# First pair of layer 0: projections, values and column sums at other places of the hand-written order

## The chip, the cores and the metric

The kernel runs on one core of a Trainium2 chip. The metric is the device time of one execution in microseconds (us). A core has five engines with queues of their own that run side by side and wait for each other by semaphores: TensorE (PE, matmuls; its weight loads are shown as PEld), VectorE (DVE), ScalarE (ACT), GpSimd (POOL), and SyncE (SP), which here issues the transfers.

## What is computed

Two layers of attention on `x` of 128 x 256 x 256 in float32, each added to its input. The change lies in layer 0 alone:

```python
m_norm = layer_norm(m)                      # m: x after a group norm over 32 groups of channels
q, k, v = m_norm @ Wq.T, m_norm @ Wk.T, m_norm @ Wv.T      # 8 heads of 32
b = layer_norm(z) @ Wb.T                    # a bias for each head, 256 x 256, the same for all rows
gate = sigmoid(m @ Wg.T + bg)
scores = einsum('bsihc,bsjhc->bshij', q, k) * scale + b
p = softmax(scores)
o = einsum('bshij,bsjhc->bsihc', p, v) * gate
x = x + o @ Wo.T + bo
```

`s` runs over 128 rows, `i` and `j` over 256 positions. Layer 1 is a banded attention on the result; nothing of it is changed.

## The kernel before

**The preparation** (up to some 219 us) reads `z` in tiles of 32 positions, forms the bias, and keeps its exponential `eb` in SBUF: exp(score + bias) is taken as exp(score) times `eb`. For a tile, VectorE takes the statistics (`zst`, L1102) and the variance (`zrs`, L1109), and POOL raises it to the power -1/2 (`z_power`, L1116). PE transposes (`z_turn`, L1143), ScalarE copies (`zT`, L1145), PE multiplies by the bias weights (`z_project`, `ps_b`, L1155). After four such steps ScalarE copies `bT` (L1164), PE transposes it back into `ps_k` (L1167), VectorE multiplies by the roots (`z_weigh`, `bt`, L1179), and ScalarE takes the exponential (`z_exp`, `eb`, L1190). Beside it, blocks of `x` are read for the mean and the root of the group norm, `M0` and `R0`.

The last tiles of `z` are woven by hand with the beginning of layer 0, in `last_tiles`. The first pair of rows, `now`, is centred and scaled on POOL (L1283, L1286), has its layer-norm statistics taken by VectorE (`moments`, L1296 to L1302), their roots by POOL (`root`, L1306), and is transposed and projected to q and k. `columns` (L1576) brings `R0` and `M0` from rows to columns: eight small PE records (L1580) and two VectorE instructions (L1584, L1585) into `col`, which pairs from the third on use in `scale_blocks`.

**The main loop** takes two rows (a pair) in each of 64 passes; in pass `p`, `now` is the pair whose scores are made, `nxt` the next, `nn` the one after it, `was` and `old` the two before. q, k and the gate of a pair are projected in two halves (`project(which, m)`, L1364) of four heads each: half 0 is enough for `scores(r, 0)`, half 1 for `scores(r, 1)`; r is the row of the pair. The steps of a pass that matter here:

- `scores(r, c)`: 8 PE matmuls (L1401) into two PSUM tiles of a pool of two, and their exponentials on ScalarE (L1413). For c = 0 the second goes to SBUF, which frees its PSUM tile.
- `add_bias(r, c)`: two products with `eb` on VectorE (`e`, L1421), and two sums over the halves of the positions on POOL (`eboth`, L1425).
- `apply(r)`: products with the values (`ps_ov`, L1436) and sums of the weights from `eboth` (`ps_su`, L1444).
- `values(r)` on PE (L1382) and `keep_values(r)` on VectorE (L1388).
- For the pair to come: `centre` and `scale` on POOL, `moments` on VectorE, `root` on POOL, `send` (a VectorE transpose, L1310, and four transfers to DRAM, L1312), `fetch` (one transfer that spreads these 512 roots over all partitions, `rs_r`, L1319), and `normal` (POOL multiplies `xgT` by `rs_r` to `xnT`, L1351).
- For pair 1, `turn`: eight PE transposes (`ps_x`, L1329) and two ScalarE copies (`xgT`, L1333). Later pairs get `xgT` by a VectorE transpose of blocks that are loaded apart (`blocks`, `turn_blocks`).
- `residual` (POOL, L1289) adds the output bias to the rows.

The order is written out by hand (`tc.manual_schedule`): each engine runs its own instructions in the order of the program text, and waits where an operand isn't there. So a step's place among other steps decides what stands behind it on each of its engines. Projections, values and the small products of `columns` share a pool of two PSUM banks (`mm`); one that finds no free bank waits for the eviction of the product two before.

In pass 0 there are no earlier pairs, so `was` and `old` do nothing, and pair 1 has to be brought from its rows to `xnT` within the pass.

Of the kernel before, what the change touches and what calls it, by code (L numbers as in the profile page):

```python
# [21 lines left out]
def bcast(ap, axis, n):  # L22

    ap = ap.unsqueeze(axis)
    shape = list(ap.shape)
    shape[axis] = n
    return ap.broadcast_to(shape)
# [746 lines left out]
def fast_kernel(  # L774
# [215 lines left out]
    def mm(name):  # L990
        return ps_mm.tile([P, 512], F32, name=name, tag="mm")
# [122 lines left out]
    def z_power():  # L1114
        rs = powers.pop(0)
        nc.gpsimd.tensor_tensor(rs, rs, mhalf[:, : rs.shape[1]], ALU.pow)  # L1116
# [57 lines left out]
    def z_weigh():  # L1174
        b, i0, rs, ps_k = unweighed.pop(0)
        bt = pz.tile([P, IS, H], F32, name="bt", tag="bt", bufs=2)
        for j in range(4):
            q = slice(j * 16, (j + 1) * 16)
            nc.vector.tensor_tensor(  # L1179
                bt[:, q, :].rearrange("p (g a) h -> p g a h", g=4), ps_k[:, :, :, j, :].rearrange("p a g h -> p g a h"),  # L1180
                bcast(rs[:, q].rearrange("p (g a) -> p g a", g=4), 3, H), ALU.mult,
            )
        weighed.append((b, i0, bt))

    def z_exp():

        while weighed:
            b, i0, bt = weighed.pop()
            for h in range(H):
                nc.scalar.activation(  # L1190
                    eb[:, h, :, b * P + i0 // NB : b * P + (i0 + IS) // NB],
                    bt[:, :, h].rearrange("p (u b) -> p b u", b=NB), AF.Exp, bias=bz_r[:, h : h + 1],
                )
# [355 lines left out]
    def pair(p):  # L1549
        return Pair(p) if p < NP else Nobody()  # L1550
# [14 lines left out]
    now = nxt = nn = None  # L1565
# [10 lines left out]
    def columns():  # L1576
        ps = mm("ps_col")
        for n, row in enumerate((R0, M0)):
            for k in range(KC):
                nc.tensor.matmul(  # L1580
                    ps[:, n * KC + k : n * KC + k + 1], row[:, k * P : (k + 1) * P], ident[:, 0:1],
                    start=True, stop=True,
                )
        nc.vector.tensor_copy(col[:, 0], ps[:, 0:KC])  # L1584
        nc.vector.scalar_tensor_tensor(col[:, 1], ps[:, KC : 2 * KC], -1.0, col[:, 0], ALU.mult, ALU.mult)  # L1585
# [3 lines left out]
    def mark():  # L1589
        if n in (1, 6):  # L1590
            next(prepare, None)

    def last_tiles(jobs):
        nonlocal la, now, nxt, nn, M0, R0
        zts = [z_load(*job) for job in jobs[:2]]
        px.release()
        la = tc.alloc_tile_pool(name="l0_early", bufs=1, side="left", reuse_waits="tile")
        now = pair(0)
        zts.append(z_load(*jobs[2]))
        s0, s1, s2 = (z_quarters(*job, zt, 2) for job, zt in zip(jobs, zts))  # L1600

        def turn(i, j):
            z_turn(*jobs[i], zts[i], zrs, j)

        next(s0)
        turn(0, 2)
        z_project()
        turn(0, 3)
        z_project()
        steps = x_moments()  # L1610
        next(steps)
        z_exp()
        next(s0)
        z_group()
        turn(1, 0)
        next(steps)
        z_project()
        next(s0)
        z_power()
        next(steps)  # L1620
        M0, R0 = next(steps)
        now.centre()
        now.scale()
        nxt = pair(1)
        next(s0)
        next(s1)
        turn(1, 1)
        z_project()
        now.moments(0)
        now.moments(1)  # L1630
        now.root()
        z_power()
        now.turn([mm("ps_x") for _ in range(KC)])
        turn(2, 2)
        now.spread_roots()
        z_project()
        next(s1)
        z_power()
        now.normal_first()
        now.project("qT", 0)  # L1640
        turn(2, 3)
        z_project()
        now.project("kT", 0)
        next(s1)
        next(s1)
        z_power()
        z_weigh()
        columns()
        z_project()
        z_exp()  # L1650
        for part in range(2):
            next(s2)
            next(s2)
            z_power()
        nn = pair(2)
        z_weigh()
        z_exp()

    behind, nx, n = None, 0, 0
    prepare = weights()  # L1660
    with tc.manual_schedule():
        zts = [z_load(*zjobs[0], 2)]
        load(8)
        zts.append(z_load(*zjobs[1]))
        for n, job in enumerate(zjobs[: xsteps[-1] + 1]):
            front = z_front(*job, zts.pop(0) if zts else z_load(*job))
            if n == 0:
                next(prepare)
                next(prepare)
            else:  # L1670
                load(4)
                if n == 1:
                    next(prepare)
            if behind is not None:
                z_back(*behind)
            behind = (*job, *front)
            if n in xsteps:
                x_block(nx)
                nx += 1
            if n == 6:  # L1680
                mark()
        z_back(*behind)
        ended = True
        last_tiles(zjobs[xsteps[-1] + 1 :])
        for f in ("centre", "scale"):
            getattr(nxt, f)()
        for r in range(2):
            nxt.moments(r)
    pps.release()
    pz.release()  # L1690
    lb = tc.alloc_tile_pool(name="l0_late", bufs=1, side="right", reuse_waits="tile")
# [5 lines left out]
    with tc.manual_schedule():  # L1697
        old = was = Nobody()
        es = nn3 = None
        for p in range(NP):  # L1700

            if p == 0:
                nxt.root()
            nxt.send()
            pss = now.scores(0, 0)
            if p == 0:
                for which in ("qT", "kT"):
                    now.project(which, 1, by_vector=True)
            e0 = now.add_bias(0, 0, pss)
            was.apply(1, es)  # L1710
            if p == 0:
                now.project("gT", 0)
            pss = now.scores(0, 1)
            was.gate(1)
            nxt.fetch()
            if p == 0:
                nxt.turn([mm("ps_x") for _ in range(KC)])
                nxt.normal()
            es = e0, now.add_bias(0, 1, pss)
            nn.centre()  # L1720
            if p > 0:
                now.project("gT", 0)
            now.values(0)
            now.keep_values(0)
            was.invert()
            was.fetch_sums()
            some(1 if p < NP - 2 else 3)
            nn.scale()
            now.project("gT", 1)
            if p > 0:  # L1730
                nxt.turn_blocks()
            nn.blocks()
            if p == 0:
                nxt.residual()
                now.residual()
            else:
                nxt.scale_blocks()
            if p < NP - 1:
                old.out_row(1)
                some(1 if p < NP - 2 else 3)  # L1740
                old.keep_row(1)
                now.values(1)
                now.keep_values(1)
            nn3 = pair(p + 3)
            if p > 0:
                nxt.normal()

            e0 = now.add_bias(1, 0, now.scores(1, 0))
            now.apply(0, es)
            pss = now.scores(1, 1)  # L1750
            now.gate(0)
            es = e0, now.add_bias(1, 1, pss)
            was.normalize(0)
            nn.moments(0)
            for m in range(KC):
                nxt.project("qT", m)
                nxt.project("kT", m)
            if p == NP - 1:
                load_first()
                old.out_row(1)  # L1760
                old.keep_row(1)
                now.values(1)
                now.keep_values(1)
                some(8)
            was.normalize(1)
            nn.moments(1)
            nn.root()
            nn.residual()
            some(3 if p < NP - 2 else 9)
            was.out_row(0)  # L1770
            was.keep_row(0)
            old, was, now, nxt, nn = was, now, nxt, nn, nn3
        was.apply(1, es)
        was.gate(1)
        was.invert()
        old.out_row(1)
        was.spread()
        old.keep_row(1)
        for r in range(2):
            was.normalize_last(r)  # L1780
        for r in range(2):
            was.out_row(r)
            was.keep_row(r)
        some(len(later))
# [29 lines left out]
    with tc.tile_pool(name="l1", bufs=2) as sb, tc.tile_pool(  # L1814
# [322 lines left out]
        with tc.manual_schedule():  # L2137
            now, nxt = pair1(0), pair1(1)
# [19 lines left out]
            for p in range(NP - 1):  # L2158
# [76 lines left out]
                was, now, nxt = now, nxt, nn  # L2235
# [107 lines left out]
```

## Time and profile before

| what | us |
|---|---|
| median of 3 runs | 3137.07 |
| lowest and highest | 3136.13, 3138.22 |
| the execution profiled | 3138.85 |
| its span, first to last instruction | 3137.1 |
| PE busy in it | 3012.3 |
| POOL busy in it | 2270.4 |

The busy time of three stretches around the change, in us, and PE's mean granted clock, from the windowed view:

```profile
205.00:215.00 10.00, 9.22 (x65) 5.03 (x63) 6.40 (x24) 5.96 (x15) 5.53 (x3) 1.00 0.00 0
215.00:260.00 45.00, 31.96 (x232) 16.75 (x231) 23.86 (x45) 18.22 (x28) 37.98 (x22) 0.89 0.14 30
260.00:305.00 45.00, 44.19 (x331) 25.55 (x330) 32.74 (x49) 22.10 (x27) 42.65 (x29) 1.00 0.36 84
```

The columns are the stretch, its length, the busy time of PE, PEld, VectorE, ScalarE and POOL with the number of instructions, the clock of PE as a share of full speed, the share of the transfer engines, and GB/s. The order of the timeline's lines is start, duration, engine, line of the program, operation, what is written from what, the number of instructions merged, and in brackets how long the engine sat idle before and what ended it. The chain of waits is followed back from the last instruction: at each step to what released it, or to the instruction before it on its engine.

### The profile page before, as it was taken

What the parts mean: (1) busy time and instruction counts of PE and PEld (TensorE: products, weight loads), DVE (VectorE), ACT (ScalarE), POOL (GpSimd) and SP (SyncE); (2) the same over time, 40 slices, a digit from 0 to 9 for tenths busy, and PEclk for the clock granted to TensorE, in tenths of its full rate; (3) what the DMA queues carried; (4) which work ended last, traced back from release to release, by engine and by line L of the source; (5) the groups of instructions that cost most, each with busy time, mean ns of one, the idle gap of its engine ahead of it and who ended that gap; (6) DMA issues with size and microseconds to landing.
All of it is one profiled execution on the core that took longest, in us unless ns stands there. A gap on an engine that the chain in (4) does not pass through costs nothing.

```text
span 3137.1 us, 80585 instructions
## 1 busy us (share of the span) xinstructions
PE 3012.3 (96%) x33630; PEld 2095.9 (67%) x33630; DVE 2401.9 (77%) x4009; ACT 1573.0 (50%) x2637; POOL 2270.4 (72%) x1635
## 2 busy tenths in 40 slices
PE   5569999999999999999999999899999999999998
PEld 3345556655555565555556555588888888888886
DVE  7976677777777777777777777588788877777788
ACT  3454444444444444444444444355555555555553
POOL 3459988988999898889988987455555555555553
PEclk9789999999999999999999999899999999999999
DMA  9952333324433432343333232544343434343431
GB/s 360 389 172 58 97 72 99 90 63 97 99 96 72 99 92 66 92 99 98 70 99 97 64 90 74 117 93 94 90 97 90 96 91 95 90 96 88 98 94 52
DMA packets 690951, 328.16 MB, mean 105 GB/s; under 512 B 538673, under 2 KB 639921, under 8 KB 689425
## 3 DMA queue, kind: packets, MB, share of 16 engines
q1 hardware_dynamic: 686176, 320.28, 40.1%
q8 instruction: 266, 4.36, 0.6%
q10 hardware_dynamic: 4400, 2.63, 0.3%
q14 instruction: 109, 0.88, 0.1%
HBM read 254.09 MB, written 68.75 MB: 103 GB/s over the span
## 4 chain that ended last, share of the span: by engine, by line
PE 90%; DMA 4%; DVE 2%; POOL 2%; issue 1%; ACT 0%; SPq 0%; POOLq 0%; DVEq 0%; ACTq 0%
PE ps_p L1364 21%; PE ps_qk L1949 12%; PE ps_sc L1401 9%; PE ps_ov L1436 7%; PE ps_su_y L2081 7%; PE ps_qk L1945 7%; PE ps_y L1491 7%; PE ps_v L1382 7%; PE ps_o L2027 4%; PE ps_su L1444 3%; PE ps_sc L2002 3%; DMA zt<-in_z_dram 2%; PE ps_su_y L2035 2%; DMA xa<-in_x_dram 1%; DVE st L1199 1%
## 5 line engine op out<-in xcount | busy, mean ns | idle before, releaser
L1425 POOL TENSOR_TENSOR eboth<-e 128x512 f32<-128x512 f32 x512 | 744.9, 1475 | 176.5 <-PE ps_su L1444 94.8
L1421 DVE TENSOR_TENSOR e<-ps_sc,eb 128x1024 f32<-128x1024 f32 x384 | 458.3, 1221 | 291.4 <-ACT ps_sc L1413 291.3
L1413 ACT ACTIVATE ps_sc<-ps_sc 128x1024 f32<-128x1024 f32 x384 | 375.4, 1007 | 436.4 <-PE ps_sc L1401 309.9
L1401 PE MATMUL ps_sc<-qT,kT 32*128 32x256 f32 x4096 | 294.1, 400 | 0.9 <-DVE e L1421 0.9
L1912 POOL TENSOR_TENSOR dT<-xgT,dT 128x256 f32<-128x256 f32 x63 | 45.9, 729 | 316.0 <-ACT xgT L1898 316.0
L1364 PE MATMUL ps_p<-xgT,wg 128*128 128x512 f32 x512 | 248.9, 609 | 10.6 <-DVE qT L1369 10.6
L2013 POOL TENSOR_TENSOR e<-e,bw 128x384 f32<-128x384 f32 x256 | 248.3, 1001 | 10.7 <-ACT e L2011 10.7
L2081 PE MATMUL ps_su_y<-w_out,oT 128*128 128x256 f32 x1008 | 254.5, 385 | 0.9 <-DVE sums L2052 0.9
L1401 PEld LDWEIGHTS ps_sc<-qT,kT 32*128 32x128 f32 x4096 | 185.3, 184 | 103.7 <-issue 92.0
L1491 PEld LDWEIGHTS ps_y<-wo,oT 128*128 128x128 f32 x1024 | 194.8, 191 | 84.2 <-issue 44.3
L1364 PE MATMUL ps_p<-xnT,wq 128*128 128x512 f32 x512 | 247.6, 606 | 0.8 <-POOL xnT L1351 0.8
L1436 PE MATMUL ps_ov<-e,v 128*32 128x256 f32 x4096 | 247.9, 382 | 0.0
L1491 PE MATMUL ps_y<-wo,oT 128*128 128x256 f32 x1024 | 243.5, 381 | 3.5 <-POOL oT L1481 2.7
L1382 PE MATMUL ps_v<-wv,xnT 128*128 128x256 f32 x1024 | 242.0, 379 | 1.6 <-ACT xgT L1333 1.6
L1364 PE MATMUL ps_p<-xnT,wk 128*128 128x512 f32 x512 | 240.7, 592 | 0.0
L1382 PEld LDWEIGHTS ps_v<-wv,xnT 128*128 128x128 f32 x1024 | 194.5, 190 | 55.9 <-issue 31.1
L2058 DVE RECIPROCAL rv<-sums 128x256 f32<-128x256 f32 x128 | 223.1, 1743 | 0.0
L1958 ACT ACTIVATE u<-ps_qk,bin_c 128x256 f32<-128x256 f32 x378 | 174.7, 477 | 95.2 <-PE ps_qk L1949 95.2
L2081 PEld LDWEIGHTS ps_su_y<-w_out,oT 128*128 128x128 f32 x1008 | 181.8, 190 | 22.4 <-DVE sums L2052 1.3
L1436 PEld LDWEIGHTS ps_ov<-e,v 128*32 128x32 f32 x4096 | 120.0, 110 | 109.0 <-issue 42.2
L1371 ACT ACTIVATE gT<-ps_p,bg_c 128x512 f32<-128x512 f32 x128 | 88.0, 687 | 184.1 <-PE ps_p L1364 184.1
L1364 PEld LDWEIGHTS ps_p<-xnT,wk 128*128 128x128 f32 x512 | 97.2, 190 | 122.8 <-issue 122.8
(231 smaller groups left out, 6557.1 us busy)
## 6 DMA issues: line engine op xcount, KB each, us to landing
xa<-in_x_dram SPq DMA_DIRECT2D x8, 4096.0 KB
xt<-in_x_dram SPq DMA_DIRECT2D x64, 512.0 KB
x<-xo SPq DMA_DIRECT2D x16, 2048.0 KB
xt<-x SPq DMA_DIRECT2D x64, 512.0 KB
rvb<-rsum SPq DMA_DIRECT2D x252, 128.0 KB
xs<-x SPq DMA_DIRECT2D x252, 128.0 KB
out_dram<-yo SPq DMA_DIRECT2D x63, 512.0 KB
xs<-in_x_dram SPq DMA_DIRECT2D x248, 128.0 KB
```

Of the source, the lines that this page charges most:

```text
L1364: nc.tensor.matmul(ps, w[:, k, m * P : (m + 1) * P], getattr(self, src)[:, k, :], start=(k == 0), stop=(k == KC - 1),)
L1382: nc.tensor.matmul(self.ps_v[:, b * C : (b + 1) * C], self.xnT[:, k, t * P : (t + 1) * P], wv[:, k, :], start=(k == 0), stop=(k == KC - 1),)
L1401: nc.tensor.matmul(self.pss[q // 2][:, q % 2, b, :], self.kT[rs, c, r * I + b * P : r * I + (b + 1) * P], self.qT[rs, c, r * I : (r + 1) * I],
L1413: nc.scalar.activation(self.pss[a], ps, AF.Exp)
L1421: nc.vector.tensor_tensor(es[a], pss[a], eb[:, h : h + 2], ALU.mult)
L1425: nc.gpsimd.tensor_tensor(t, es[a][:, :, 0, :], es[a][:, :, 1, :], ALU.add)
L1436: nc.tensor.matmul(ov[q * D0 : (q + 1) * D0, c, :], self.v[:, r, b, h * D0 : (h + 1) * D0], es[q // 2][:, q % 2, b, :], start=(b == 0), st ...
L1491: nc.tensor.matmul(self.ps_y[:, b * C : (b + 1) * C], self.oT[r][:, k, b * P : (b + 1) * P], wo[:, k, :], start=(k == 0), stop=(k == KC - 1),)
L1949: nc.tensor.matmul(to, lhs, rhs, start=start, stop=True, skip_group_check=True)
L2013: nc.gpsimd.tensor_tensor(e[:, q], e[:, q], bcast(bw.rearrange("p b w -> p (b w)"), 1, KC), ALU.mult)
L2058: nc.vector.reciprocal(self.rv[:, r, :], self.sums)
L2081: nc.tensor.matmul(self.y[:, b], self.oT[r][:, k, b * P : (b + 1) * P], w_out[:, k, :], start=(k == 0), stop=(k == KC - 1),)
```

## The change

In the preparation, half 1 of q and k of the first pair is projected before the second-last bias is weighed and before the last bias is projected, with evictions on ScalarE; before, it was projected in the main loop behind the first scores, with evictions on VectorE. `columns` moves behind the last bias exponential. The statistics of pair 1 move from the end of the preparation, and its root and `send` from the head of pass 0, behind `add_bias(0, 0)` of pass 0. Both rows of values of pair 0 move ahead of that `add_bias`, the second with its eviction behind it. `normal` of pair 1 moves behind `add_bias(0, 1)`. The other passes keep their order.

```diff
         next(s1)
         next(s1)
         z_power()
+        now.project("qT", 1)
+        now.project("kT", 1)
         z_weigh()
-        columns()
         z_project()
         z_exp()
         for part in range(2):
...
         nn = pair(2)
         z_weigh()
         z_exp()
+        columns()
...
         for f in ("centre", "scale"):
             getattr(nxt, f)()
-        for r in range(2):
-            nxt.moments(r)
...
-            if p == 0:
-                nxt.root()
-            nxt.send()
+            if p > 0:
+                nxt.send()
             pss = now.scores(0, 0)
             if p == 0:
-                for which in ("qT", "kT"):
-                    now.project(which, 1, by_vector=True)
+                now.values(0)
+                now.keep_values(0)
+                now.values(1)
             e0 = now.add_bias(0, 0, pss)
             was.apply(1, es)
             if p == 0:
+                now.keep_values(1)
+                for r in range(2):
+                    nxt.moments(r)
+                nxt.root()
+                nxt.send()
                 now.project("gT", 0)
             pss = now.scores(0, 1)
             was.gate(1)
             nxt.fetch()
             if p == 0:
                 nxt.turn([mm("ps_x") for _ in range(KC)])
+            es = e0, now.add_bias(0, 1, pss)
+            if p == 0:
                 nxt.normal()
-            es = e0, now.add_bias(0, 1, pss)
             nn.centre()
             if p > 0:
                 now.project("gT", 0)
-            now.values(0)
-            now.keep_values(0)
+                now.values(0)
+                now.keep_values(0)
...
-                now.values(1)
-                now.keep_values(1)
+                if p > 0:
+                    now.values(1)
+                    now.keep_values(1)
```

## The prediction

> **What bounds the kernel now.** The page first: PE is busy 96% of the span, so only the stretches where PE waits can pay. The chain of waits, in order of time, says where the chain runs on PE without a break: from 273.14 us on. A shift of that point shifts the end. Before it, from 213.63 to 273.05 us, nearly every piece is POOL's.
>
> ```profile
> PE 3012.3 (96%) x33630; PEld 2095.9 (67%) x33630; DVE 2401.9 (77%) x4009; ACT 1573.0 (50%) x2637; POOL 2270.4 (72%) x1635
> ...
> 219.39 2.32 POOL xg L1283
> 221.77 2.34 POOL xg L1286
> ...
> 226.13 1.01 POOL lrs L1306
> ...
> 250.74 4.92 POOL eboth L1425 x4
> 255.66 0.99 POOL lrs L1306
> 256.88 3.17 DVE e L1421 x2
> ```
>
> The timeline of POOL alone in 185 to 275 us gives its order and its holes (in brackets: idle before, and what ended it):
>
> ```profile
> 213.63 5.76 POOL L1116 TENSOR_TENSOR zrs<-zrs,mhalf 128x16 f32<-128x16 f32 x2 [4.47 <-DVE zrs L1109]
> ...
> 226.12 1.01 POOL L1306 TENSOR_TENSOR lrs<-lrs,mhalf 128x4 f32<-128x4 f32 x1 [2.00 <-DVE lrs L1302]
> 229.87 3.40 POOL L1425 TENSOR_TENSOR eboth<-e 128x512 f32<-128x512 f32 x2 [2.75 <-DVE e L1421]
> 235.39 2.50 POOL L1351 TENSOR_TENSOR xnT<-xgT,rs_r 128x512 f32<-128x512 f32 x2 [2.12 <-ACT xgT L1333]
> 237.85 2.49 POOL L1425 TENSOR_TENSOR eboth<-e 128x512 f32<-128x512 f32 x2
> ```
>
> Four holes: 4.47 + 2.00 + 2.75 + 2.12 = 11.34 us; from 235.39 to 273.05 there is none. The timeline of PE shows the large idle time that the change attacks, and the two later places where PE still waits:
>
> ```profile
> 228.06 3.66 PE L1364 MATMUL ps_p<-xgT,wg 128*128 128x512 f32 x4 [10.63 <-DVE qT L1369]
> ...
> 258.04 1.13 PE L1401 MATMUL ps_sc<-qT,kT 32*128 32x256 f32 x12 [0.86 <-DVE e L1421]
> ...
> 273.14 1.13 PE L1364 MATMUL ps_p<-xnT,wq 128*128 128x512 f32 x2 [0.81 <-POOL xnT L1351]
> ```
>
> The reader is to see that PE loses 10.63 us at 217.4 to 228.06, but meets POOL twice afterwards: at 258.04 (the first product of pass 1, which stands on VectorE behind the transpose of pair 2's roots, which POOL finished at 256.6), and at 273.14. So the gain is what POOL gains by 256.6, not what PE gains at 228.
>
> [...]the eboth pair took 3.40 us beside the product e<-e,eb (229.71 to 230.93) and 2.49 us beside none. [...]after the 10.63 us the four gT records took 3.66 us, 1.88 us elsewhere. [...]four root sends leave at 227.40 to 228.72 and the fetch, which waits for them, is issued at 229.71 only.
>
> **The change, part by part,** along the queues, times on before's clock.
>
> *Preparation, PE and ScalarE.* Projecting q and k for half 1 moves from behind the first scores to ahead of the last bias projection: two projections of two matmuls each (four records), 1.72 us a projection when they follow one another (249.15 to 250.87). wk of half 0 is issued until 209.34, so the two end at 212.78; the bias projection, before at 210.22, starts there. ScalarE copied bT 1.21 us after that start, so now at 213.99 (its two new evictions, 0.69 us each, are done at 213.7); ps_k follows at 214.6 instead of 212.06. The columns come last: 0.88 us of PE, 215.2 to 216.1, then the scores 1.08 us to 217.2 (before 212.65 to 213.73). By itself this is 3.5 us later, but the scores wasted 8.4 us before their exponential at 222.10.
>
> *Preparation, VectorE and POOL.* VectorE idled 3.49 us for the columns at 210.32. With them last, the eight z statistics start at 206.8, and the two z powers of POOL at 209.79 instead of 213.63 (POOL is free at 209.16). They take 5.76 us, to 215.55; centring and scaling pair 1 take 4.76 us, to 220.27 (before 224.11). The last bt needs ps_k (215.3) and the last power: 216.2. ScalarE: first bias exponential 214.5 to 216.8, second to 219.2 (2.35 us each), score exponentials at 219.2 and 220.1, 1.00 us each (before 222.10).
>
> *First pass, VectorE.* Two tensor_scalar evictions (0.71 + 0.74) leave. The order is now: columns 216.2 to 216.6, values 0 (PE 217.2 to 219.0) at 219.15, product at 220.27 and 221.40, values 1 at 222.54 (PE had it at 220.8), pair 1's statistics at 223.15 (before 224.15, where they stood first). Root on POOL 1.97 us later: 225.12. Transpose 226.16, send 226.40, 1.0 us earlier than 227.40. The fetch on SP, 2.31 us after, is at 228.71; its packets ended 3.12 us after issue before, and the semaphore of the sends needed 0.44 us: row of roots at 232.25. The block loads and pair 3's load stand behind it on SP and move by the same 1.0 us; they are used from 259 us on, so cost nothing.
>
> *First pass, PE.* Values to 220.7, gT half 0 to 222.4, scores (0,1) to 223.6, transposes to 224.6, gT half 1 from 226.15 (it needs a bank that the copy of xgT frees), scores (1,0) done 229.6, all without the 10.63 us and at full clock. Before they ended at 241.8: PE is 12 us ahead, and will wait.
>
> *First pass, POOL, which counts.* eboth(0,0) follows the first product at 221.56[...] (3.40 us): 224.96. Root 225.12 to 226.13. Product (0,1) follows the transpose at 226.29 to 227.50, eboth(0,1) 227.58 to 230.07, which now precedes the normalising. That waits for the row: 232.25. New holes: 209.16 to 209.79, 0.63; 220.27 to 221.56, 1.29; 0.16; 1.45; 230.07 to 232.25, 2.18; sum 5.71. The work is the same, so POOL gains 11.34 - 5.71 = **5.6 us**. Product (1,0) half 1, all in SBUF, before cost POOL 0.9 us beside the residuals (5.67 for two, 2.38 for the single one); now it falls at 231.95 to 233.15, on the normalising. I take the same 0.9; if it is over before the row lands the gain is 6.5.
>
> *Pass 1.* From 232.25 POOL has no hole: 17.71 us (235.39 to 255.59 less the 2.49 that moved ahead) to the root of pair 2 at 249.96. PE has done pair 1's projections by 241.8, scores and apply by 244.65, then its sum matmuls wait one by one for the four eboth (246.3 to 250.0) and the second scores for the product at 252.4 (before 258.04, again 5.6). In 244.65 to 252.4 PE does some 2.5 us of work, a third. The windowed view shows the clock halved after windows with PE busy 0.31, 0.33 and 0.42, not after 0.44, and restored after 0.84, not after 0.75. So I expect it halved here, where before PE was busy throughout. From 252.4 it stays slow[...], of which half is lost: 1.4 to 3.0, middle 2.2. PE's wait of 0.81 at 273.14 absorbs as much: 1.4 us net (0.6 to 2.2).
>
> **Sum:** 5.6 - 1.4 = 4.2 us. The execution profiled took 3138.85 us for a span of 3137.1, 1.75 outside, which the change doesn't touch; it stands 1.8 above the median 3137.07. Against the median: 3132.9.
>
> **Rivals.**
> *The clock holds.* For it: small matmuls keep arriving every 1.25 us[...]. Against: a third of busy time, below all cases that held. Gain 5.6[...]: 3131.5 (3130.6).
> *PE is the bound.* Then 10.63 us and the 1.8 of slow clock go, 12.4: 3124.7. For it: 96% busy, and the wait named. Against: the waits at 258.04 and 273.14, and POOL without a hole from 235.39.
> *The gain is lost in the row of roots.* If the row comes no earlier[...], normalising starts at 234.4 instead of 232.25, the gain is 3.5 less 1.4 to 2.2 of clock: 3135.5.
> *Slower.* Pair 1's statistics now stand on VectorE behind two products that wait for the last bias, and root, send, fetch, normalising and all of pass 1 stand behind them. Each microsecond by which the first product is later than 220.27 is paid in full; at 224.5 the gain of 4.2 is gone. Should the last bias reach the products 11 us late, at 231, it is 3143.8. For it: the projections delay bT by 2.6 us and the exponentials form one chain on ScalarE. Against: every link has a measured duration, and the data of z had landed before 190 us (DMA share 0.35 in 190 to 192, nothing from 194 on).
>
> **How the numbers follow.** Chances: forecast 0.50, clock holds 0.27, PE the bound 0.10, row of roots 0.07, slower 0.06. 0.2% is 6.3 us, about what a measurement of this kernel can tell from no change. Faster by more: all of PE the bound, half of the clock that holds (5.6 to 6.5 and some noise), and 0.06 of the forecast's edge: 0.29. Slower: 0.06. Within: 0.65. Range 3130 to 3136: from [...] to the late row, outside it PE the bound and slower, 0.16.
>
> **What would show it.** POOL's two z powers at 209.8 with no 4.47 us hole; pair 1's root at 225 and its send at 226.4; normalising near 232.3 with a DMA as releaser in place of ScalarE's copy; pair 2's root near 250; no 10.63 us on PE, but several waits of about 1 us for POOL in 244 to 252 and a halved clock after them. The prediction is wrong if the product of pass 1 doesn't lie 5.6 us earlier, if the clock stays full, or if the first product starts after 224.

## The result, and the profile after

The changed kernel takes 3133.5 us (median of 20 runs, 3129.34 to 3134.36), the kernel before in the same session 3137.32 (20 runs, 3136.13 to 3139.7): a ratio of 0.9985, interval 0.9978 to 0.9992. Measured again later, beside another experiment, it was 3132.53 against 3138.43, 0.9982 (0.9974 to 0.9990). Both intervals leave out 1, so the gain is real: 3.8 and 5.9 us, or 0.12% and 0.19%.

PE's waits in 205 to 276 us of the changed kernel (in total us, times, longest):

```profile
PE ps_su L1444 <- POOL eboth L1425: 2.7, 4, 1.4
PE ps_p L1364 <- ACT xgT L1333: 1.6, 1, 1.6
PE ps_p L1364 <- POOL xnT L1351: 1.4, 1, 1.4
```

The 10.63 us for VectorE's eviction of q are gone. The wait for ScalarE's copy of `xgT` stood in the kernel before too, as did one of 0.7 us for `bT`. New are the waits for POOL, four of them for the sums of the weights. In pass 0, PE is 12.2 us ahead of its old place. Its first products with the values, before:

```profile
241.81 1.93 PE L1436 MATMUL ps_ov<-e,v 128*32 128x256 f32 x32
```

and after:

```profile
229.61 1.93 PE L1436 MATMUL ps_ov<-e,v 128*32 128x256 f32 x32
```

The timeline of POOL alone shows why so little came of it:

```profile
209.71 5.77 POOL L1116 TENSOR_TENSOR zrs<-zrs,mhalf 128x16 f32<-128x16 f32 x2 [0.62 <-DVE zrs L1109]
...
221.46 3.41 POOL L1425 TENSOR_TENSOR eboth<-e 128x512 f32<-128x512 f32 x2 [1.24 <-DVE e L1421]
224.99 1.02 POOL L1306 TENSOR_TENSOR lrs<-lrs,mhalf 128x4 f32<-128x4 f32 x1
227.44 2.50 POOL L1425 TENSOR_TENSOR eboth<-e 128x512 f32<-128x512 f32 x2 [1.43 <-DVE e L1421]
233.51 2.50 POOL L1351 TENSOR_TENSOR xnT<-xgT,rs_r 128x512 f32<-128x512 f32 x2 [3.58 <-DMA rs_r<-rs_d]
...
240.71 4.69 POOL L1289 TENSOR_TENSOR xt<-xt,bo_r 128x1024 f32<-128x1024 f32 x2
245.36 4.92 POOL L1425 TENSOR_TENSOR eboth<-e 128x512 f32<-128x512 f32 x4
250.25 1.02 POOL L1306 TENSOR_TENSOR lrs<-lrs,mhalf 128x4 f32<-128x4 f32 x1
```

The z powers start at 209.71 instead of 213.63, and POOL's holes have shrunk by 4.3 us, from 11.34 to 7.0; one of them, 3.58, is now a wait for the row of roots. Another 1.0 us comes from the two residuals, 4.69 instead of 5.67. Pair 2's root stands at 250.25 instead of 255.59: POOL gained 5.34 us. The timeline of PE behind it:

```profile
243.34 1.93 PE L1436 MATMUL ps_ov<-e,v 128*32 128x256 f32 x32
246.67 0.63 PE L1444 MATMUL ps_su<-eboth,pick 128*32 128x256 f32 x4 [1.39 <-POOL eboth L1425]
...
250.34 1.07 PE L1444 MATMUL ps_su<-eboth,pick 128*32 128x256 f32 x4 [0.16 <-POOL eboth L1425]
251.33 3.41 PE L1401 MATMUL ps_sc<-qT,kT 32*128 32x256 f32 x16
254.68 3.78 PE L1364 MATMUL ps_p<-xgT,wg 128*128 128x512 f32 x4
...
274.14 1.45 PE L1364 MATMUL ps_p<-xnT,wk 128*128 128x512 f32 x3
```

PE reached these sums at 245.3, 10 us ahead of their old place, and stood still for POOL; then its clock was halved (0.50 from 248.72 to 258.96), and the gate projection took 3.78 us instead of 1.98. The windowed view of the same kernel shows the clock in the last column but two:

```profile
244.50:248.50 4.00, 2.01 (x24) 0.50 (x16) 0.00 (x0) 0.89 (x1) 4.00 (x4) 1.00 0.02 4
248.50:252.50 4.00, 3.25 (x14) 0.88 (x12) 1.20 (x2) 0.00 (x0) 4.00 (x4) 0.53 0.00 0
252.50:259.00 6.50, 6.39 (x20) 3.36 (x19) 5.03 (x5) 2.43 (x3) 6.50 (x5) 0.50 0.12 41
```

A fixed mark tells how much of POOL's 5.34 us reached PE's unbroken stretch: the start of pair 2's last k projection. Before:

```profile
277.54 1.88 PE L1364 MATMUL ps_p<-xnT,wk 128*128 128x512 f32 x4
```

It is at 274.14 now, 3.40 us earlier; the missing 1.94 are put down to the clock, and E3 and E10 test this. From that mark to the end the profiled execution of before took 2859.6 us and that of the changed kernel 2858.5. In all the executions profiled in this study, this remainder varied between 2856.4 and 2860.8 where nothing in it was changed, so a single execution doesn't show a difference of 1 to 2 us at its end, while the mark does. The traces show where it varies. The last output product of layer 0 starts 1708.3 to 1708.5 us behind the mark in eight of these eleven executions, the two kernels among them, so a gain at the mark is still there at the end of layer 0. In the other three (E2, E5, E7) it is 1706.8 or 1706.9. The two kernels have the clock halved for 3.41 us near the end of layer 0 (from 1972.26 us before, from 1969.04 after), which at half speed costs, by estimate from this length, up to 1.7 us, about the 1.6 us by which the three are shorter. Layer 1, in which no run changed anything, takes 1149.5 to 1152.3 us.

### The profile page after: what moved, and what is told of

Its sections match the earlier page's. It is cut to its first block, busy times and chain, and to the rows that moved or that the text cites. A ratio compares the mean times of both kernels' runs of the same rounds, so it can differ in the third digit from the quotient of the medians.

```text
span 3132.6 us, 80584 instructions
## 1 busy us (share of the span) xinstructions
PE 3017.0 (96%) x33630; PEld 2096.3 (67%) x33630; DVE 2398.1 (77%) x4007; ACT 1574.6 (50%) x2639; POOL 2271.3 (73%) x1635
## 4 chain that ended last, share of the span: by engine, by line
PE 90%; DMA 4%; DVE 3%; issue 1%; POOL 1%; ACT 1%; SPq 0%; POOLq 0%; ACTq 0%; DVEq 0%
PE ps_p L1364 22%; PE ps_qk L1956 12%; PE ps_sc L1401 9%; PE ps_ov L1436 7%; PE ps_su_y L2088 7%; PE ps_v L1382 7%; PE ps_qk L1952 7%; PE ps_y L1491 7%; PE ps_o L2034 4%; PE ps_su L1444 3%; PE ps_sc L2009 3%; PE ps_su_y L2042 2%; DMA xa<-in_x_dram 1%; DVE st L1199 1%; DMA zt<-in_z_dram 1%
```

## The experiments

All are timed beside the kernel before. "The mark" is the start of pair 2's last k projection in the profiled execution.

**E1. Only the column sums last**, from the kernel before:

```diff
         z_weigh()
-        columns()
         z_project()
...
         z_weigh()
         z_exp()
+        columns()
```

> The kernel before, with one step moved: the column sums stand behind the last bias exponential. Theory A (the time follows POOL up to the root of pair 2): the two z powers start 3.8 us earlier (209.8 instead of 213.6), and everything from centring pair 1 on moves with them, so 3137.3 - 3.8 = 3133.5 us, PE's wait for VectorE's eviction of q falls from 10.6 to about 6.8 us. Theory B (the time follows the wait of PE that the change removes, 10.6 us and 1.8 of slow clock): also 3.8 us less, by the same shift. The run tells how much of the change this one line is: if A holds, nearly all of it.

Measured: 3134.44 us, ratio 0.9990 (0.9982 to 0.9998). POOL's timeline:

```profile
222.51 1.01 POOL L1306 TENSOR_TENSOR lrs<-lrs,mhalf 128x4 f32<-128x4 f32 x1 [2.00 <-DVE lrs L1302]
226.26 3.40 POOL L1425 TENSOR_TENSOR eboth<-e 128x512 f32<-128x512 f32 x2 [2.75 <-DVE e L1421]
231.50 2.50 POOL L1351 TENSOR_TENSOR xnT<-xgT,rs_r 128x512 f32<-128x512 f32 x2 [1.84 <-ACT xgT L1333]
```

The holes of 2.00, 2.75 and 1.84 us (before 2.12) stand 3.6 to 3.9 us earlier; pair 2's root is at 251.73 and the mark at 273.63, both 3.9 us earlier. PE's wait for the eviction of q fell to 5.99 us. Two instructions of 0.16 us on VectorE, moved behind sixteen statistics, are worth more at the mark (3.91) than the whole change (3.40), and 3.0 of its 3.8 us in the median. In these traces the rest of the change wins POOL 1.5 us more (root at 250.25) and loses 1.94 at the mark. The run doesn't tell the theories apart.

**E2. Only the projections early**, from the kernel before:

```diff
         z_power()
+        now.project("qT", 1)
+        now.project("kT", 1)
         z_weigh()
         columns()
...
-                for which in ("qT", "kT"):
-                    now.project(which, 1, by_vector=True)
```

> The kernel before, with one step moved: half 1 of q and k of the first pair is projected in the preparation, evicted by ScalarE; the column sums stay ahead of the last bias projection. The wait of 10.6 us on PE is gone. Theory A (POOL): POOL's z powers, centring and root stay where they are; the first product starts 1.3 us earlier without the two evictions by VectorE, and normalising waits for the row of roots at 233.3 to 234.5 instead of 235.4, so at most 2 us are won and up to 1.4 lost to a halved clock in pass 1: 3135.3 to 3137. Theory B (PE): 10 to 12 us less, 3126.

Measured: 3138.39 us, ratio 1.0003 (0.9995 to 1.0011): no gain. From PE's timeline:

```profile
227.57 1.22 PE L1401 MATMUL ps_sc<-qT,kT 32*128 32x256 f32 x4 [8.46 <-ACT e L1413]
232.01 2.08 PE L1401 MATMUL ps_sc<-qT,kT 32*128 32x256 f32 x12 [3.22 <-DVE e L1421]
```

The wait for the eviction of q is gone, but PE now waits at the next scores: 8.46 us for ScalarE's exponential, which frees a PSUM tile, and 3.22 us for VectorE's product. That is 11.7 us, against 12.2 before (10.63 and 1.55). So the run didn't take PE's waiting away, as was expected of it, and does not decide against theory B. It shows that the early projections alone win nothing. What decides is the changed kernel itself: there PE was 12.2 us ahead in pass 0, and the mark moved by 3.40. Theory A was off as well, at one place. POOL's timeline:

```profile
217.10 5.76 POOL L1116 TENSOR_TENSOR zrs<-zrs,mhalf 128x16 f32<-128x16 f32 x2 [7.90 <-DVE zrs L1109]
```

The z powers did not stay where they were: the column sums, still ahead of the statistics on VectorE, now stood behind the two projections on PE, and POOL's z powers came 3.5 us later. The first pass won back a part (pair 2's root 256.90, the mark 278.82, both 1.3 us later than before).

**E3 and E10. PE kept busy in pass 1**, from the changed kernel; the added products are read by nobody:

```diff
+            if p == 1:
+                for _ in range(3):
+                    ps = mm("ps_w")
+                    for k in range(KC):
+                        nc.tensor.matmul(ps, wg[:, k, 0:P], now.xgT[:, k, :], start=(k == 0), stop=(k == KC - 1))
             was.apply(1, es)
```

> The changed kernel with work added that nobody reads: three projections (six matmuls of 128 x 512, 5.2 us) on PE in pass 1 between the first scores and the apply, where PE waits for POOL (243.3 to 250). Theory A (the clock is halved for want of work there and costs 2 to 3 us): the clock stays full, 3131 us, and the runs lie closer together than 3129.3 to 3134.4. Theory C (the halved clock is hidden by waits for POOL or is a matter of the records): 3133.5, no change. If the added work itself delays PE, up to 1 us more.

Measured in E3: 3132.52 us (3130.2 to 3134.41), ratio 0.9984 (0.9978 to 0.9991). The windowed view of E3, same columns:

```profile
244.50:248.50 4.00, 4.00 (x13) 1.54 (x11) 0.00 (x0) 0.68 (x1) 4.00 (x4) 1.00 0.00 0
248.50:252.50 4.00, 3.46 (x57) 1.79 (x56) 1.42 (x3) 0.00 (x0) 4.00 (x4) 1.00 0.02 4
252.50:259.00 6.50, 6.50 (x30) 3.99 (x31) 6.50 (x6) 2.63 (x4) 6.50 (x5) 1.00 0.12 41
```

The clock is full, and the mark is at 271.95, 5.59 us earlier than before, which is what POOL gained there (5.58, pair 2's root at 250.01). So at the mark the halved clock costs about 2 us, and 5.4 us of useless matmuls won it back. The executions were expected to lie closer together than the changed kernel's; they did only a little (4.2 us from lowest to highest, against 5.0). As the two medians came from different sessions, both kernels were run once more side by side:

> The changed kernel itself, on the same chip and in the same rounds as the next run, since the earlier difference of 1.0 us between the two came from different sessions. Theory A (the halved clock of pass 1 costs up to 2.2 us[...]): 3133.5 us, with executions in a range of some 5 us. Theory C (no cost of the clock): the same time as the next run within 0.3 us.

> The changed kernel with three projections that nobody reads in PE's idle time of pass 1, side by side with the changed kernel. Theory A: 1 to 2 us below it. Theory C: within 0.3 us.

Measured: E9, the changed kernel, 3132.53 us (14 runs, 3130.39 to 3135.53); E10, with the added matmuls, 3132.73 (19 runs, 3131.41 to 3135.09). No difference in the time, which is theory C's figure, not theory A's. The traces repeat the first pair: in E9 the clock was at half speed over 252.5 to 259.0 and the mark at 274.76, 1.73 us less gained than by POOL (root at 251.08, 4.51); in E10 it was full, the mark at 272.21, as much gained as by POOL (5.33 and 5.29). But E10's remainder behind the mark took 2860.8 us, E9's 2858.6. In this pair it is layer 1 that took the difference back: at the last output product of layer 0, E10 is still 2.4 us ahead (1980.7 against 1983.1), and layer 1 takes 1152.3 us instead of 1150.3. So the loss at the mark is shown in two pairs of traces, and the medians don't show it. Other executions of the changed kernel may escape the halved clock. Only profiled executions show the clock by place, but each has a mean clock on record: 9 of the 34 executions of the changed kernel stand at 0.987 or 0.988 and have a median of 3131.0 us, the other 25 at 0.985 or 0.986 with 3133.7; with the added matmuls 36 of 40 stand at 0.987 or 0.988, with 3132.5. This fits, but is a correlation and no test.

**E4. Pair 1's roots spread by PE**, from the changed kernel; pair 1 is normalised by VectorE from PSUM, as pair 0 is:

```diff
                 nxt.root()
-                nxt.send()
...
-            nxt.fetch()
+            if p > 0:
+                nxt.fetch()
             if p == 0:
                 nxt.turn([mm("ps_x") for _ in range(KC)])
+                nxt.spread_roots()
             es = e0, now.add_bias(0, 1, pss)
             if p == 0:
-                nxt.normal()
+                nxt.normal_first()
```

> The changed kernel, with pair 1's roots spread by PE (four small matmuls into PSUM) and its normalising done by VectorE from there, as pair 0 does it, in place of four sends, a fetch and POOL's two products. POOL loses the hole of 3.6 us before normalising and its 2.5 us of work. Theory A (POOL to the root of pair 2): that root comes at 244.2 instead of 250.25, 6.1 us less, and with the shorter wait in pass 1 the clock stays full, 2 us more: 3125.5 us. Theory B (PE's own waits in pass 0 and 1, 5.6 us in all, decide): 3128 at best. Theory D (pair 1's row of roots is not on the path): 3133.5.

Measured: 3126.0 us (5 runs, 3123.88 to 3127.75), ratio 0.9963 (0.9949 to 0.9976), 11.4 us below before. It beats both kernels. POOL's timeline has no hole from the second sums on:

```profile
227.23 2.50 POOL L1425 TENSOR_TENSOR eboth<-e 128x512 f32<-128x512 f32 x2
229.68 2.37 POOL L1283 TENSOR_TENSOR xg<-xt,M_l 128x1024 f32<-128x1024 f32 x1
...
245.00 1.02 POOL L1306 TENSOR_TENSOR lrs<-lrs,mhalf 128x4 f32<-128x4 f32 x1
```

Pair 2's root is at 245.00, 5.25 us earlier than in the changed kernel (its preparation ended 1.1 us later in this execution, so that 6.4 us lie behind the root of pair 1), and the clock stayed full (the first gate projection of pass 1 took 1.98 us). The mark is at 266.93, 7.2 us earlier. Theory D, no change, falls. Theory B gave 3128 at best, which lies inside the interval (some 3121 to 3130 us), so the time alone doesn't rule it out. The mark speaks for POOL: against the kernel before, its root came 10.59 us earlier and the mark 10.61.

**E5. Useful work in PE's hole**, from the changed kernel: both rows of values of pair 1 and their evictions ahead of `apply` in pass 1.

```diff
+            if p == 1:
+                for r in range(2):
+                    now.values(r)
+                    now.keep_values(r)
             was.apply(1, es)
```

(and `p > 1` where they stood).

> The changed kernel, with both rows of values of pair 1 (3.5 us of PE, their evictions too) moved in pass 1 from behind the gate projections into the time in which PE waits for POOL. Theory A (POOL's chain holds until pair 2's normalised rows at 267.5): as with the added work that nobody reads, 3132.5 us: the clock stays full, and PE waits some 3 us more for pair 2's rows instead of working. Theory B (PE is the bound from pass 1 on): 3.5 us less than that, 3129.

Measured: 3131.76 us (13 runs), ratio 0.9980 (0.9972 to 0.9988), 0.7 us from theory A's figure and 2.8 from B's. From PE's timeline:

```profile
255.20 5.40 PE L1364 MATMUL ps_p<-xgT,wg 128*128 128x512 f32 x8 [1.52 <-DVE v L1388]
...
268.38 1.12 PE L1364 MATMUL ps_p<-xnT,wq 128*128 128x512 f32 x2 [0.99 <-POOL xnT L1351]
```

PE, with 3.5 us less to do there, waited for the evictions of the values and again for pair 2's rows. Theory A's full clock did not come: it was halved from 255.3 to 258.7, and a part of the waiting came as slow clock.

**E6. Normalising ahead of the second bias product**, as before, the rest as changed (the two statements exchanged).

> The changed kernel with the normalising of pair 1 ahead of the second bias product again, as before. Theory A: POOL has nothing to do while the row of roots is under way, and the two sums of the second bias product (2.5 us) come behind it: pair 2's root at 252.8 instead of 250.25, 2.5 us later; 3136 us. Theory B: PE needs the sums 2.5 us later in pass 0 but waits anyway, no change.

Measured: 3134.68 us (13 runs, 3131.83 to 3137.53), ratio 0.9988 (0.9980 to 0.9996). POOL stood still 6.56 us for the row of roots instead of 3.58, and pair 2's root came at 251.85, 1.6 us later than in the changed kernel; behind the row, normalising began 0.8 us earlier in this execution (232.68 instead of 233.51), which makes up the rest of the 2.5 but 0.1. So the place of `normal` behind the sums is worth 1.6 to 2.4 us at the root; the medians, 3134.68 and 3133.5 from different sessions, don't show it clear of the noise.

**E7. Column sums back ahead of the last bias projection**, the rest as changed.

> The changed kernel with the column sums back ahead of the last bias projection. VectorE waits for them behind the two new projections, until about 213.8, and the two z powers start at 216.6 instead of 209.7. Theory A: centring, root and all that follows on POOL lie some 6 us later than in the changed kernel, less what POOL had as holes there (1.2 us): 3138 us, the gain is gone. Theory B: PE has other work in that time, 3134.

Measured: 3140.29 us (13 runs, 3136.57 to 3142.72), ratio 1.0008 (1.0000 to 1.0017): all of the gain gone, and 2 us more. POOL's timeline of the fastest of these runs:

```profile
217.03 5.76 POOL L1116 TENSOR_TENSOR zrs<-zrs,mhalf 128x16 f32<-128x16 f32 x2 [7.90 <-DVE zrs L1109]
...
239.79 2.49 POOL L1351 TENSOR_TENSOR xnT<-xgT,rs_r 128x512 f32<-128x512 f32 x2 [3.48 <-DMA rs_r<-rs_d]
...
256.49 1.02 POOL L1306 TENSOR_TENSOR lrs<-lrs,mhalf 128x4 f32<-128x4 f32 x1
```

The z powers wait 7.90 us, and pair 2's root lies 6.2 us behind that of the changed kernel. The delay was 7.3 us at the z powers and 6.2 at the root, where 6 less 1.2 had been expected. The mark of this fastest execution is at 278.41, 4.3 us later than in the changed kernel. With E1 this settles the part of the column sums: moved alone they win 3 us, and without this move the other parts win nothing, since the early projections make the column sums wait (as in E2).

**E8. Output bias of pairs 0 and 1 later**, from E4:

```diff
             if p == 0:
-                nxt.residual()
-                now.residual()
...
             if p > 0:
                 nxt.normal()
+            if p in (1, 2):
+                was.residual()
```

> The kernel with pair 1's roots spread by PE, and the output bias of pairs 0 and 1 added on POOL in passes 1 and 2 behind the normalising instead of in pass 0 (5.7 us of POOL leave the stretch before pair 2's root). Theory A: POOL is no longer what PE waits for, PE's last two waits of 0.9 and 0.8 us shorten, and PE bounds from pass 0 on: up to 1.7 us less than 3126, 3124.5. If POOL were still the bound, 5.7 us less, 3120.5; if the deferred work comes back in pass 1 or 2, no gain or a loss of up to 2 us.

Measured: 3129.17 us (8 runs), ratio 0.9973 (0.9962 to 0.9983): 8.8 us below before, where E4 was 11.4 below. The root of pair 2 came at 240.26 and PE's two waits were gone, but the deferred work came back. From PE's timeline:

```profile
268.43 2.91 PE L1491 MATMUL ps_y<-wo,oT 128*128 128x256 f32 x8 [2.16 <-POOL oT L1481]
...
298.66 1.99 PE L1491 MATMUL ps_y<-wo,oT 128*128 128x256 f32 x8 [0.97 <-POOL oT L1481]
```

In passes 1 and 2 the output products waited for POOL's normalised rows, and behind the first, of 2.16 us, the clock was halved (269.4 to 272.8; eight output records took 2.91 us, behind the second wait 1.99). That is the last of the three outcomes expected, with a loss somewhat over the 2 us set for it.

## Why the prediction was right

- *The bound.* The mechanism was right: the time follows POOL to pair 2's root, not PE's wait. PE was 12.2 us ahead in pass 0 of the changed kernel and gained 3.40 at the mark; E4 took work and a wait from POOL and gained 7.5 us more. In the six traces in which the clock is full from pass 1's gate projection on, the mark moved with this root. Us earlier than before, root and mark: E1 3.86 and 3.91, E2 -1.31 and -1.28, E3 5.58 and 5.59, E4 10.59 and 10.61, E7 -0.90 and -0.87, E10 5.29 and 5.33. It ends where POOL's work is put off: in E8 the root is 15.3 us earlier, the mark 13.2.
- *Preparation.* Its steps came within 0.15 us: z powers 209.71 (forecast 209.79), first product 220.16 (220.27), pair 1's root 224.99 (225.12), send 226.28 (226.40).
- *Row of roots.* Mis-sized: 3.54 us were forecast from fetch to normalising, and it took 4.93, 228.58 to 233.51. Normalising began 1.3 us behind the forecast, and 2.1 in E9 (234.38). By the updates of its semaphore in the two kernels' traces, the row lands in 16 parts. In the kernel before, the last part landed 3.65 us after issue: the transfer itself was sized about right. In the changed kernel fifteen parts had landed after 3.35, and the last after 4.43. During this row the changed kernel's trace has one packet of 16 KB in a queue of the kind `instruction`, from 1.05 to 2.77 us after the issue; the trace of before has none there. That this packet held the last part up was not shown: no run moved it. The last 0.50 us, from landing to the start of POOL's first product, the forecast put at nothing. Of the 0.99 us between the last send of before and its fetch, 0.44 lie behind the last packet of the sends.
- *VectorE's product beside POOL's work.* Mis-sized the other way: 0.9 us were charged for VectorE's product of two SBUF operands; it ran at 231.51 to 232.73 in POOL's wait for the row, and cost POOL nothing (the two residuals 4.69 instead of 5.67). The pair of sums of the first product took 3.41 us, again with such a product beside it (221.30 to 222.52), the next pair, with none beside it, 2.50: here the 3.40 and 2.49 us of before came back.
- *POOL's sum.* 5.6 forecast, 5.34 measured (4.51 in E9), and pass 1's product 5.38 earlier (251.43 instead of 256.81). That it came so close is luck: the row was 1.3 us too long, the two residuals gave back 1.0.
- *The clock.* Forecast halved for want of work while PE waits for the sums, 1.4 us net (0.6 to 2.2): 1.94 and 1.73 at the mark. Cause and size are right there (with the added matmuls of E3 and E10 the clock stayed at 1.00); in the medians of E9 and E10 the loss is not to be seen. In the 3.41 us before the clock fell, PE was busy 1.25, a share of 0.37, below the 0.42 that the prediction read from before. That the slow clock would cost 1.4 to 3.0 us was the author's estimate. It was slow for 10.24 us, and stayed at 0.50 behind stretches of 3.41 us with PE busy 2.87 and 3.30, shares of 0.84 and 0.97, so that the 0.84 after which it came back in before doesn't hold here.
- *The sum.* 4.2 us forecast; 3.40 and 2.78 at the mark, 3.8 and 5.9 between medians. The part behind the mark, which the prediction took as unchanged, varies by more than the difference. So the medians don't separate the forecast from the rival of the clock that holds (5.6 us); the traces do.
- *The rivals.* PE as the bound (12.4 us) fell with the changed kernel itself. The clock that holds was E3 and E10: its local gain is there, its time within the spread. The lost row of roots came half true (233.51, between 232.25 and 234.4). The slower case showed its mechanism in E7, with one difference: the chain that was late was the z powers behind the column sums, not the last bias.

## What to carry to other kernels

The longest wait of the busiest engine was worth only what the next engine in its chain left of it (10.63 us on PE, 3.40 at the mark): add up what that engine's holes and its work shrink by, up to the place where the two meet again, and take this sum as the gain. A wait that is removed can come back at the next instruction (12.2 us in before, 11.7 in E2), so see in the trace that it is gone. A small instruction in a strict queue is priced by what stands behind it (two of 0.16 us were worth 3 to 6). When work is pulled ahead on PE and the other engine isn't, the new idle time may come out as a halved clock (here 1.94 and 1.73 us at the mark), so compare a fixed event in the trace, and then the medians.

## What the runs showed of the hardware

- A row of 256 KB issued by SyncE had landed 3.65 us after issue in the trace of before. In the changed kernel 15 of its 16 parts had landed after 3.35 us and the last after 4.43. Four sends of 0.5 KB were followed by the fetch 2.31 and 2.30 us after the first issue.
- PE's clock was halved in the changed kernel with small matmuls still running every 1.2 us (PE busy 2.01 of the 4 us from 244.5 on), not only when PE was idle. It stayed so for 10.24 us in the changed kernel's trace, 6.8 in E9 and 3.4 in E5.
- The remainder of some 2858 us behind the mark varied by 4.4 us between executions of kernels that don't differ there: 1.6 us of it in layer 0, 2.8 us within layer 1.
